# Turning self attention's output through DRAM and VectorE instead of TensorE, in a decoder layer on one core

## The chip, the core and the metric

The kernel runs on one core of one Trainium2 chip. The metric is the device time of one execution in microseconds; the median of 3 runs of the kernel before is 2142.93 (2141.88 to 2144.9). Its engines are TensorE (PE: matmuls; PEld: its weight loads), VectorE (DVE), ScalarE (ACT), GpSimd (POOL) and SyncE (SP), which only issues DMAs here. Each engine works through its own instructions in order, and waits on semaphores for the others.

## The reference

One decoder layer with its normalization behind each part, in fp32: self attention with relative positions, cross attention over a context, and a feed-forward part with its weights and hidden values rounded to 8 bits. x is (8, 512, 512). The first axis is the sequence here (8 positions) and the second is a batch of 512, so self attention has 8 keys for each of 16 heads of 32.

```python
qkv = x @ in_proj_weight.T + in_proj_bias
q, k, v = jnp.split(qkv, 3, axis=-1)             # each (t, b, h, d), t = 8, b = 512
p = (pos @ pos_proj_weight.T + pos_proj_bias).reshape(-1, h, d)
ac = jnp.einsum('tbhd,sbhd->bhts', q + r_w_bias, k)
bd = _rel_shift(jnp.einsum('tbhd,rhd->bhtr', q + r_r_bias, p))[..., :t]
attn = jax.nn.softmax((ac + bd) * scale, axis=-1)
ctx = jnp.einsum('bhts,sbhd->tbhd', attn, v).reshape(t, b, e)
x = _layernorm(x + ctx @ out_proj_weight.T + out_proj_bias)
...
x = _layernorm(x + cross_attention(ctx_2048, x, mask))
x = _layernorm(x + ffn(x))
```

The change concerns `ctx` and its product with `out_proj_weight`.

## The kernel before, in words

There are two stages, one after the other. The first does self attention and the keys and values of the context (1024 features) for cross attention; the second does cross attention and the feed-forward part. Only the first is touched.

**Self attention.** A loop over j = 0..3 takes 128 of the 512 batch rows at a time, one a partition, and within it loops over the 8 positions t. Keys (L232), queries (L373) and values (L410) come from TensorE through `project` (L214). As every batch row has its own 8 keys, scores and weighted sums are not matmuls but VectorE work: `pq` (L387) multiplies q by all keys and `sc` (L396) sums it, both in two halves (g) of eight heads. Behind the softmax (L415 to L427) comes the loop over t that the change is in. For each t, VectorE multiplies the values by the weights (`pv`, L436) and adds the eight products pairwise in three steps (L446, L449, L452), again in two halves; the last step writes one half of `ao`, 128 rows x 512 features. For the output product the features have to be on the partitions, so TensorE turns the four 128x128 blocks of `ao` (L457) into the PSUM bank `aot`, ScalarE copies them to `aoT` (L459), and TensorE multiplies by `w_o` into `po` (L462). x comes from DRAM as `r` (L471; a ring of 4) and GpSimd adds the bias (L472); VectorE adds `po` (L478) and takes statistics (L100, L101). After every fourth t the four rows are normalized (L111) and stored to `x1d` by ScalarE's queue; the ring's slots then load the next four x.

**Context.** Six of the eight contexts go in pairs (m = 0..2) through a Strassen-Winograd scheme with seven products a block instead of eight (L552; banks `py`, `pz`, `px` of the pool `a_kv`; sums of the operands on VectorE at L142 to L145, of the results at L594). In the first pass over the weights (keys) the sums of the context are also stored to DRAM (`td`, L529 and L530), in the second (values) they are loaded from there (L532, L533). Context chunks `ch` (L520) and `cl` stay in a ring of 8. Context 6 goes through the plain products `psk` (L160) and `psv` (L174), its weights `w6k` and `w6v` lying where k_all and v_all were: `w6v` can load once the last `pv` product has read v_all. Context 7 belongs to the second stage.

**What sets the order.** In the first stage the tile framework orders each engine's instructions by its own estimate of times: the context's matmuls are laid between those of self attention. All loads of the stage, and the stores to `td`, stand in one order on SP's queue, where a DMA that waits holds up those behind it. PSUM has 8 banks: 2 for projections, 1 each for `bd`, `aot` and `po`, 3 for the context.

In the second stage the order is written out by hand. It starts with the load of `x1Ts`, block-wise from `x1d` (`load_blocks`, L746), turned in place by VectorE (L752); its memory lies partly where a tile of context 6 was, which the last tile of `psv` reads. The products `psq` (L824) follow.

Of the kernel before, what the change touches and what calls it, by code (L numbers as in the profile page):

```python
# [9 lines left out]
F32 = mybir.dt.float32  # L10
# [5 lines left out]
PSUM = bass.MemoryType.PSUM  # L16

P = 128
E = 512
EC = E // P  # L20
# [22 lines left out]
def decoder_layer(  # L43
# [22 lines left out]
    nc = tc.nc  # L66
# [5 lines left out]
    ident = const.tile([P, P], F32, name="ident")  # L72
# [8 lines left out]
    def col(i):  # L81
# [3 lines left out]
    dram = ctx.enter_context(  # L85
        tc.tile_pool(name="dram", bufs=1, space=bass.MemoryType.DRAM)
    )
# [101 lines left out]
    with ExitStack() as ph:  # L189
# [5 lines left out]
        bo = wa.tile([P, E], F32, name="bo")  # L195
        ps_mm = ph.enter_context(tc.tile_pool(name="a_mm", bufs=2, space=PSUM))
        ps_bd = ph.enter_context(tc.tile_pool(name="a_bd", bufs=1, space=PSUM))
        ps_tr = ph.enter_context(tc.tile_pool(name="a_tr", bufs=1, space=PSUM))
        ps_o = ph.enter_context(tc.tile_pool(name="a_o", bufs=1, space=PSUM))
        ps_kv = ph.enter_context(tc.tile_pool(name="a_kv", bufs=3, space=PSUM))  # L200

        xtp = ph.enter_context(tc.tile_pool(name="xtp", bufs=8))
        kvp = ph.enter_context(tc.tile_pool(name="kvp", bufs=1))
        qp = ph.enter_context(tc.tile_pool(name="qp", bufs=2))
# [18 lines left out]
        def keys_of(j):  # L223

            k_all = kvp.tile([P, T, E], F32, tag="k", name=f"k{j}")
            xts = []
            for t in range(T):
                xt = xtp.tile([P, EC, P], F32, tag="xt", name=f"xt{j}_{t}")
                nc.sync.dma_start(xt, xT[t, j])
                xts.append(xt)  # L230
                ps = project(xt, 1, f"k{j}_{t}")
                nc.scalar.copy(k_all[:, t, :], ps)  # L232
            return xts, k_all
# [129 lines left out]
        for j in range(NJ):  # L363
            xts, k_all = first if j == 0 else keys_of(j)
            v_all = kvp.tile([P, T, E], F32, tag="v", name=f"v{j}")
            sc = kvp.tile([P, T, P], F32, tag="sc", name=f"sc{j}")

            for t in range(T):  # L370
                ps = project(xts[t], 0, f"q{j}_{t}")
                qw = qp.tile([P, E], F32, tag="qw", name=f"qw{j}_{t}")
                nc.vector.tensor_tensor(qw, ps, bqw, ALU.add)  # L373
                if t % 4 == 0:
                    bd = ps_bd.tile([P, 4, H1, T], F32, tag="bd", name=f"bd{j}_{t}")
                for e in range(EC):
                    nc.tensor.matmul(
                        bd[:, t % 4],
                        lhsT=xts[t][:, e, :],
                        rhs=gp[:, e, :, 7 - t : 15 - t],  # L380
                        start=(e == 0),
                        stop=(e == EC - 1),
                    )
                for g in range(2):
                    fs = slice(g * HW, (g + 1) * HW)
                    pr = prp.tile([P, HH, T, D1], F32, tag="pr", name=f"pq{j}_{t}_{g}")
                    nc.vector.tensor_tensor(  # L387
                        pr,
                        qw[:, fs]
                        .rearrange("p (h d) -> p h d", d=D1)  # L390
                        .unsqueeze(2)
                        .to_broadcast([P, HH, T, D1]),
                        k_all[:, :, fs].rearrange("p s (h d) -> p h s d", d=D1),
                        ALU.mult,
                    )
                    nc.vector.tensor_reduce(  # L396
                        sc[:, t, g * HH * T : (g + 1) * HH * T],
                        pr.rearrange("p h s d -> p (h s) d"),
                        AX.X,
                        ALU.add,  # L400
                    )
                if t % 4 == 3:
                    half = sc[:, t - 3 : t + 1, :].rearrange("p t s -> p (t s)")
                    nc.vector.tensor_tensor(
                        half, half, bd.rearrange("p t h s -> p (t h s)"), ALU.add
                    )

            for t in range(T):
                ps = project(xts[t], 2, f"v{j}_{t}")
                nc.scalar.copy(v_all[:, t, :], ps)  # L410


            for t in range(T):
                row = sc[:, t, :].rearrange("p (h s) -> p h s", s=T)
                nc.gpsimd.tensor_tensor(row, row, gc[:, :, 7 - t : 15 - t], ALU.add)  # L415
            sc3 = sc.rearrange("p t (h s) -> p (t h) s", s=T)
            red = sm.tile([P, T * H1], F32, tag="red", name=f"mx{j}")
            nc.vector.tensor_reduce(red, sc3, AX.X, ALU.max)
            nc.vector.tensor_tensor(
                sc3, sc3, red.unsqueeze(2).to_broadcast([P, T * H1, T]), ALU.subtract  # L420
            )
            nc.scalar.activation(sc3, sc3, AF.Exp, scale=1.0 / math.sqrt(D1))
            den = sm.tile([P, T * H1], F32, tag="red", name=f"den{j}")
            nc.vector.tensor_reduce(den, sc3, AX.X, ALU.add)
            rden = sm.tile([P, T * H1], F32, tag="rden", name=f"rden{j}")
            nc.vector.reciprocal(rden, den)
            nc.vector.tensor_tensor(  # L427
                sc3, sc3, rden.unsqueeze(2).to_broadcast([P, T * H1, T]), ALU.mult
            )

            for t in range(T):
                ao = qp.tile([P, E], F32, tag="ao", name=f"ao{j}_{t}")
                for g in range(2):
                    fs = slice(g * HW, (g + 1) * HW)
                    pr = prp.tile([P, T, HH, D1], F32, tag="pr", name=f"pv{j}_{t}_{g}")
                    nc.vector.tensor_tensor(  # L436
                        pr,
                        v_all[:, :, fs].rearrange("p s (h d) -> p s h d", d=D1),
                        sc[:, t, g * HH * T : (g + 1) * HH * T]
                        .rearrange("p (h s) -> p s h", s=T)  # L440
                        .unsqueeze(3)
                        .to_broadcast([P, T, HH, D1]),
                        ALU.mult,
                    )
                    pf = pr.rearrange("p s h d -> p s (h d)")
                    nc.vector.tensor_tensor(  # L446
                        pf[:, 0:4, :], pf[:, 0:4, :], pf[:, 4:8, :], ALU.add
                    )
                    nc.vector.tensor_tensor(  # L449
                        pf[:, 0:2, :], pf[:, 0:2, :], pf[:, 2:4, :], ALU.add  # L450
                    )
                    nc.vector.tensor_tensor(ao[:, fs], pf[:, 0, :], pf[:, 1, :], ALU.add)  # L452

                pt = ps_tr.tile([P, E], F32, tag="tr", name=f"aot{j}_{t}")
                for c in range(EC):
                    cs = slice(c * P, (c + 1) * P)
                    nc.tensor.transpose(pt[:, cs], ao[:, cs], ident)  # L457
                aoT = qp.tile([P, E], F32, tag="aoT", name=f"aoT{j}_{t}")
                nc.scalar.copy(aoT, pt)  # L459
                po = ps_o.tile([P, E], F32, tag="po", name=f"po{j}_{t}")  # L460
                for c in range(EC):
                    nc.tensor.matmul(  # L462
                        po,
                        lhsT=aoT[:, c * P : (c + 1) * P],
                        rhs=w_o[:, c, :],
                        start=(c == 0),
                        stop=(c == EC - 1),
                    )
                xin = rp.tile([P, E], F32, tag="r", name=f"r{j}_{t}")
                n0 = t * NB + j * P  # L470
                nc.sync.dma_start(xin, x[n0 : n0 + P, :])  # L471
                nc.gpsimd.tensor_tensor(xin, xin, bo, ALU.add)  # L472
                if t % 4 == 0:
                    mvs = sm.tile([P, 4, 2], F32, tag="mv1", name=f"mva{j}_{t}")
                    rts = []
                r = xin
                rts.append(r)
                nc.vector.tensor_tensor(r, po, r, ALU.add)  # L478
                stats_of(sm, mvs[:, t % 4, :], r, f"a{j}_{t}")
                if t % 4 == 3:  # L480
                    rs = rstd_of(sm, mvs, 4, f"a{j}_{t}")
                    for i in range(4):
                        normalize(rts[i], rts[i], mvs, rs, i)
                        nc.scalar.dma_start(x1d[t - 3 + i][j], rts[i])
# [141 lines left out]
        t = T - 2  # L626
# [735 lines left out]
```

## Time and profile before

| | |
|---|---|
| median of the runs | 2142.93 us |
| profiled execution, its own time | 2141.88 us |
| its span on the core | 2140.0 us |
| TensorE, busy | 2067.8 us (97%) |
| VectorE, busy | 1434.3 us (67%) |
| ScalarE, busy | 464.1 us (22%) |
| GpSimd, busy | 167.7 us (8%) |
| DMA, mean over the span | 119 GB/s |
| granted TensorE clock, mean | 0.989 |
| last `ao` of the first stage ends at | 833.70 us |
| load of `x1Ts` issued at | 887.70 us |

Busy time is the time in which at least one instruction of the engine runs; ends of matmuls are modelled, and consecutive ones overlap, so TensorE's share is an upper bound. A row of groups gives line, engine, operation, output and inputs by name, shape and count, then busy time and mean duration. An issue row of a DMA ends with its size and the median time from issue to landing. A row of waits reads: who waited for whom, total us, times, longest. A timeline row starts with start and duration.

### The profile page before, as it was taken

Reading aid. Unit: us, or ns where it says so; the run is one execution under the profiler, and the core shown is the slowest. Engines: PE = TensorE matmul, PEld = TensorE weight load, DVE = VectorE, ACT = ScalarE, POOL = GpSimd, SP = SyncE. Lnnn points to the kernel's source line nnn. Section 1 sums busy time; section 2 is a strip of 40 time slices with the busy share of each in tenths; the row PEclk is TensorE's granted clock in tenths of the full one; section 3 lists DMA queues with packets and bytes.
Section 4 is the critical chain, followed back from the end, with each engine's and each line's share of the span. In section 5 each row is a group of like instructions: output and inputs, shape, how many; then the busy total and the mean of one; then the engine's idle time right before and its main releaser. Section 6 shows DMA issues by size and latency. Waiting matters only on the chain.

```text
span 2140.0 us, 17293 instructions
## 1 busy us (share of the span) xinstructions
PE 2067.8 (97%) x5776; PEld 887.8 (41%) x5776; DVE 1434.3 (67%) x2290; ACT 464.1 (22%) x955; POOL 167.7 (8%) x148
## 2 busy tenths in 40 slices
PE   8999999999999999888999999999999999999998
PEld 5444444444444444333334443434444434443443
DVE  2999999999999996055763664845746648356332
ACT  3011101110110111122233232232332322323211
POOL 0100120011011001101101011010010100000000
PEclk9999999999999999999999999999999999999999
DMA  6510644134025345765484563844646537436200
GB/s 213 211 44 24 222 147 143 40 134 145 16 67 198 122 152 177 200 165 124 107 202 118 106 141 70 144 105 99 133 104 111 135 80 152 97 75 148 60 20 20
DMA packets 246201, 255.26 MB, mean 119 GB/s; under 512 B 141025, under 2 KB 161505, under 8 KB 246113
## 3 DMA queue, kind: packets, MB, share of 16 engines
q1 hardware_dynamic: 229888, 225.55, 41.3%
q10 hardware_dynamic: 16224, 28.61, 3.7%
q8 instruction: 46, 0.75, 0.1%
q14 instruction: 43, 0.34, 0.1%
HBM read 130.36 MB, written 56.62 MB: 87 GB/s over the span
## 4 chain that ended last, share of the span: by engine, by line
PE 65%; DVE 26%; DMA 5%; issue 2%; SPq 1%; POOL 1%; ACT 0%; ACTq 0%; DVEq 0%; POOLq 0%
PE h L1033 21%; PE pox L978 5%; PE s L844 5%; PE psq L824 5%; PE pox L966 5%; PE av L944 5%; DVE pv L436 5%; DVE sc L396 4%; PE o L1050 4%; DVE pq L387 4%; PE px L552 3%; DVE pv L446 3%; PE psk L160 3%; PE psv L174 2%; DVE pv L449 2%
## 5 line engine op out<-in xcount | busy, mean ns | idle before, releaser
L1033 PE MATMUL h<-x2T,w 128*128 128x512 f32 x1024 | 454.5, 599 | 4.4 <-DVE x2T L752 4.4
L1033 PEld LDWEIGHTS h<-x2T,w 128*128 128x128 f32 x1024 | 192.1, 191 | 263.2 <-issue 255.1
L859 DVE CUSTOM_DVE_ANT_0 pe<-s,mb 128x512 f32<-128x512 f32 x256 | 162.1, 681 | 206.7 <-PE s L844 206.7
L869 ACT ACTIVATE pe<-pe,nmax 128x512 f32<-128x512 f32 x256 | 182.2, 713 | 231.8 <-DVE nmax L859 230.0
L896 DVE STREAM_TRANSPOSE pb<-pe 128x512 f32<-128x512 f32 x256 | 159.5, 678 | 0.0
L1040 ACT ACTIVATE hq<-h,colv 128x512 fp8e4<-128x512 f32 x128 | 88.0, 687 | 296.8 <-PE h L1033 296.8
L436 DVE TENSOR_TENSOR pv<-v,sc 128x2048 f32<-128x2048 f32 x64 | 149.5, 2336 | 2.0
L387 DVE TENSOR_TENSOR pq<-qw,k 128x2048 f32<-128x2048 f32 x64 | 147.9, 2311 | 1.0
L396 DVE TENSOR_REDUCE sc<-pq 128x64 f32<-128x2048 f32 x64 | 146.0, 2282 | 1.4
L844 PE MATMUL s<-kT,qTx 64*128 64x512 f32 x512 | 130.0, 625 | 5.4 <-DVE nmax L859 5.3
L824 PE MATMUL psq<-x1Ts,w_tgt 128*128 128x512 f32 x256 | 119.2, 620 | 13.3 <-DVE x1Ts L752 13.3
L944 PE MATMUL av<-pT,vx 128*64 128x512 f32 x512 | 119.2, 608 | 7.0 <-DMA pT<-pb 5.7
L214 PE MATMUL ps_q<-w_in,xt 128*128 128x512 f32 x256 | 119.4, 598 | 0.4 <-DVE qw L373 0.4
L884 DVE TENSOR_SCALAR pe<-pe,rden 128x512 f32<-128x512 f32 x256 | 116.5, 497 | 4.5
L462 PE MATMUL po<-w_o,aoT 128*128 128x512 f32 x256 | 118.7, 607 | 0.0
L978 PE MATMUL pox<-w_xo,uT 128*128 128x512 f32 x256 | 115.2, 598 | 0.0
L966 PE MATMUL pox<-w_xo,x1Ts 128*128 128x512 f32 x256 | 115.0, 598 | 0.0
L214 PE MATMUL ps_k<-w_in,xt 128*128 128x512 f32 x256 | 115.0, 599 | 0.0
L1050 PE MATMUL o<-w2q,hq 128*128 128x512 fp8e4 x512 | 114.1, 379 | 0.0
L214 PE MATMUL ps_v<-w_in,xt 128*128 128x512 f32 x256 | 112.0, 594 | 0.0
L985 DVE TENSOR_TENSOR x<-pox,x 128x512 f32<-128x512 f32 x32 | 22.1, 692 | 106.4 <-PE pox L978 68.5
L552 PE MATMUL px<-tx,w 128*128 128x512 f32 x192 | 89.0, 595 | 3.0 <-DVE st L594 3.0
(147 smaller groups left out, 2136.8 us busy)
## 6 DMA issues: line engine op xcount, KB each, us to landing
pT<-pb SPq DMA_DIRECT2D x512, 128.0 KB, 2.3
ch<-in_ctxT_dram SPq DMA_DIRECT2D x24, 512.0 KB, 5.7
td<-tx SPq DMA_DIRECT2D x12, 768.0 KB, 6.0
tx<-td SPq DMA_DIRECT2D x12, 768.0 KB, 9.3
xt<-in_xT_dram SPq DMA_DIRECT2D x32, 256.0 KB, 2.7
r<-in_x_dram SPq DMA_DIRECT2D x32, 256.0 KB, 3.7
x1d<-r ACTq DMA_DIRECT2D x32, 256.0 KB, 2.5
x1Ts<-x1d SPq DMA_DIRECT2D x32, 256.0 KB, 5.9
```

Of the source, the lines that this page charges most:

```text
L214: nc.tensor.matmul(ps, lhsT=xt[:, e, :], rhs=w_in[:, e, part * E : (part + 1) * E], start=(e == 0), stop=(e == EC - 1),)
L387: nc.vector.tensor_tensor(pr, qw[:, fs] .rearrange("p (h d) -> p h d", d=D1) .unsqueeze(2) .to_broadcast([P, HH, T, D1]), k_all[:, :, fs]. ...
L396: nc.vector.tensor_reduce(sc[:, t, g * HH * T : (g + 1) * HH * T], pr.rearrange("p h s d -> p (h s) d"), AX.X, ALU.add,)
L436: nc.vector.tensor_tensor(pr, v_all[:, :, fs].rearrange("p s (h d) -> p s h d", d=D1), sc[:, t, g * HH * T : (g + 1) * HH * T] .rearrange( ...
L824: nc.tensor.matmul(ps, lhsT=w_tgt[:, e, o * P : (o + 1) * P], rhs=x1T[t][:, e, :], start=(e == 0), stop=(e == EC - 1),)
L844: nc.tensor.matmul(ps[:, h, :], lhsT=qT[t][half[h], c, j * P : (j + 1) * P], rhs=kT[t, c][half[h], :], start=True, stop=True,)
L869: nc.scalar.activation(pe, pe, AF.Exp, bias=nmax[:, h : h + 1], scale=-1.0, accum_out=den[:, h : h + 1],)
L944: nc.tensor.matmul(av[half[h], :], lhsT=v[t, c][:, s, half[h]], rhs=pT[t, c][:, :, :, s, h].rearrange("p g i q -> p (g i) q"), start=(s == 0),
L966: nc.tensor.matmul(po, lhsT=x1T[t][:, e, j * P : (j + 1) * P], rhs=w_xo[:, e, :], start=(e == 0), stop=False,)
L978: nc.tensor.matmul(po, lhsT=uT[t][:, e, j * P : (j + 1) * P], rhs=w_xo[:, EC + e, :], start=False, stop=(e == EC - 1),)
L1033: nc.tensor.matmul(ps, lhsT=w1[0][:, e, n * P : (n + 1) * P], rhs=x2T[t][:, e, :], start=(e == 0), stop=(e == EC - 1),)
L1050: nc.tensor.matmul(po, lhsT=hq[t][:, c, j * P : (j + 1) * P], rhs=w2q[:, c, :], start=(c == 0), stop=(c == HC - 1),)
```

## The change

In the loop over t of the weighted sums, `ao` is stored to a DRAM tile of its own (`aod`), and loaded back in four DMAs, all on SP's queue. The DMA for a fills the partitions 32a to 32a + 31 with the features of that quarter of each 128-feature chunk, taken in 32x32 blocks: 512 runs of 32 elements, 128 B each. One VectorE instruction then transposes each 32x32 block of `aoT` in place, which completes the turn, and the output product reads `aoT` as before. `aoT` gets three buffers instead of two. TensorE's transposes, their PSUM bank and ScalarE's copy go; the bank goes to the pool of the context's products, which has four instead of three. In the changed program the lines behind the edit lie seven further (output product L469, transpose L466, store L457, block loads L460).

```diff
-        ps_tr = ph.enter_context(tc.tile_pool(name="a_tr", bufs=1, space=PSUM))
         ps_o = ph.enter_context(tc.tile_pool(name="a_o", bufs=1, space=PSUM))
-        ps_kv = ph.enter_context(tc.tile_pool(name="a_kv", bufs=3, space=PSUM))
+        ps_kv = ph.enter_context(tc.tile_pool(name="a_kv", bufs=4, space=PSUM))
...
-                pt = ps_tr.tile([P, E], F32, tag="tr", name=f"aot{j}_{t}")
-                for c in range(EC):
-                    cs = slice(c * P, (c + 1) * P)
-                    nc.tensor.transpose(pt[:, cs], ao[:, cs], ident)
-                aoT = qp.tile([P, E], F32, tag="aoT", name=f"aoT{j}_{t}")
-                nc.scalar.copy(aoT, pt)
+                aod = dram.tile([P, E], F32, name=f"aod{j}_{t}")
+                nc.sync.dma_start(aod, ao)
+                aoT = qp.tile([P, E], F32, tag="aoT", bufs=3, name=f"aoT{j}_{t}")
+                for a in range(4):
+                    nc.sync.dma_start(
+                        aoT[32 * a : 32 * a + 32].rearrange(
+                            "p (c g e) -> p c g e", c=EC, e=32
+                        ),
+                        aod.rearrange("(g r) (c a e) -> a r c g e", r=32, a=4, e=32)[a],
+                    )
+                nc.vector.transpose(aoT, aoT)
                 po = ps_o.tile([P, E], F32, tag="po", name=f"po{j}_{t}")
```

## Prediction

> **What bounds the kernel now.** I read the page's first two parts, then the waits and windows of the first 900 us (the change sits there), then the timeline of a few tiles, and last the order in which the changed program's instructions stand on each engine, beside that of the old one.
>
> The page says TensorE is 97% busy, which hides where the change falls. In the 40 slices (53.5 us each) VectorE is full from the second to the fifteenth and thins out after:
>
> ```profile
> PE   8999999999999999888999999999999999999998
> DVE  2999999999999996055763664845746648356332
> ```
>
> Windows, whose columns are length, then busy time and instructions of PE, PEld, DVE, ACT and POOL, PEclk, DMA share and GB/s:
>
> ```profile
> 53.00:838.00 785.00, 757.26 (x2011) 344.17 (x2011) 740.54 (x664) 95.61 (x153) 73.69 (x65) 1.00 0.34 119
> 838.00:896.00 58.00, 55.64 (x130) 24.32 (x128) 3.66 (x8) 7.51 (x11) 3.44 (x2) 1.00 0.69 207
> ```
>
> VectorE works 740.5 of 785 us. TensorE's 757 overstates it: a 128x512 matmul record lasts 0.6 us but the next starts 0.43 us later, so the stage's 1600 records of that size (768 of L214, 256 of L462, 576 of L552) are 688 us, the 256 of L377 at 0.11 another 28. VectorE is the tighter engine; of its 44 us of idle time 31 have a name and lie before the last ao, half of them inside the softmax (columns: total, times, longest):
>
> ```profile
> DVE den L424 <- ACT sc L422: 8.6, 4, 2.5
> DVE mx L418 <- POOL sc L415: 7.1, 4, 1.8
> DVE r L478 <- PE po L462: 5.9, 2, 5.1
> DVE r L478 <- POOL r L472: 5.2, 4, 1.7
> DVE st L594 <- PE px L552: 4.8, 4, 3.6
> ```
>
> From 838 to 896 only TensorE works, on context 6 (psk, psv). The last ao ends at T = 833.70; the load of x1Ts that opens the second stage is issued at 887.70, T + 54.0. Since the orders from psq on are the same in both programs, the change is worth what it does to T plus what it does to that tail.
>
> **The change part by part.**
>
> *Taken off TensorE:* 128 transposes of 128x128, a record every 0.11 us: 14 us. With them go its weight loads' waits for ao (27.8 us) and for aoT (15.4 us). TensorE is not what T waits for, so I book nothing, except that VectorE's waits on px and po may shrink: -2 us of the 5.6 that they make without the 5.1 that fell after T. *Taken off ScalarE:* 32 copies of 587 ns, on an engine at 22%: nothing. *The fourth bank* lets products start earlier: nothing while VectorE sets T.
>
> *Added to VectorE:* 32 transposes of 128x512, 31 of them before T in the new order. The nearest row is the same operation on the same shape:
>
> ```profile
> L752 DVE STREAM_TRANSPOSE x1Ts<-x1Ts x32: 667/670/711, 898.3 to 1797.7; 128x512 f32<-128x512 f32 x32
> ```
>
> A rule speaks for the full price: the Trainium skill, "VectorE: DVE Perf Modes", section on the DRAIN, says the next operation does not start until the pipe has emptied. That makes 31 x 0.67 = 20.8 us. The trace disagrees where an independent operation is put between two dependent ones, which is where most of these stand:
>
> ```profile
> 372.72 1.23 DVE L446 TENSOR_TENSOR pv<-pv 128x1024 f32<-128x1024 f32 x1
> ...
> 375.17 2.29 DVE L436 TENSOR_TENSOR pv<-v,sc 128x2048 f32<-128x2048 f32 x1
> 377.38 0.68 DVE L478 TENSOR_TENSOR r<-po,r 128x512 f32<-128x512 f32 x1
> 377.98 1.22 DVE L446 TENSOR_TENSOR pv<-pv 128x1024 f32<-128x1024 f32 x1
> ```
>
> L446 starts 2.81 us after its L436 with r between and 2.33 without (370.39 to 372.72): r starts 0.08 before its predecessor ends and the next 0.08 before r does, so its 0.68 costs 0.48. About 23 transposes stand so (0.48); 8 stand beside another inserted operation, where only the later overlap helps (0.60). I take 31 x 0.51 = +15.8 us.
>
> *Moved past T:* r, its statistics and aggregate for j=3, t=6 come after the last ao now (before, at 829.6). By the same timeline the three together cost 10.49 - 9.54 = 0.95 us a t: -1.0 us.
>
> *Added to SP's queue:* 32 stores of 256 KB and 128 block loads of 64 KB, each first load waiting for its store to land, with everything behind it on SP waiting too. Rows for 256 KB each (last column: us from issue to landing), the first two in runs of 2 KB, the third in runs of 128 B like the block loads:
>
> ```profile
> xt<-in_xT_dram SPq DMA_DIRECT2D x32, 256.0 KB, 2.7
> ...
> x1d<-r ACTq DMA_DIRECT2D x32, 256.0 KB, 2.5
> x1Ts<-x1d SPq DMA_DIRECT2D x32, 256.0 KB, 5.9
> ```
>
> The Trainium skill, "DMA: Bandwidth & Descriptors", Specifications, wants at least 512 B a run for full rate; the loads have 128 B. It gives no price, the rows do: 256 KB in 128 B runs land 3.2 us later than in 2 KB runs, a quarter of it is 0.8; raw<-vd, 64 KB in 512 B runs, lands in 2.2 us and takes 0.44 to issue. So a block load is 3.0 us and a turned tile is ready 2.5 + 4 x 0.44 + 3.0 = 7.3 us after ao. From above: four issues at x1Ts's own median, 1.4 us, and its 5.9 give 14.0 us. I take 7.3, as 64 KB is nearer to raw's size.
>
> What hides it: in the new order 11.6 us of VectorE's operations or more stand between an ao and its transpose (13.9 to 16.3 for about half), about 11 by the overlap above. At 7.3 us it costs nothing; past 11 the transpose holds up every pv product behind it in VectorE's order. From the transpose to the add of r there are 4.65 us, and po takes 3.7 from a free TensorE: covered.
>
> Where other issues stand between, I work out what is late:
> - j=0, t=4: SP's order has two context loads (ch, cl) between the store and the block loads; cl waits for the buffer's last reader, seven products (6.0 us) behind po of t=3 (3.5). So it issues 9.7 us after the transpose of t=3 and lands 6.6 later by its row, the block loads behind it no sooner: 16.3, and VectorE asks at 13.8: +2.5 us.
> - j=1, t=4: six stores of sums to td (3.75 MB; 1.2 us each to issue) stand before the load of r of t=4, which also needs a normalized row's store. Counted from the sum that frees the first store, the normalized row is stored at 13, r lands 3.7 later and has bo added in 1.7: 18.4; VectorE asks at 15.8: +2.6.
> - the other loads of r behind SP's new waits, and po where TensorE is just inside a matmul: +2, my estimate.
>
> Together with the -2 above: +5 us. From below -9 (no new stall, and the 5.6 of px and po and the 3.3 of tx gone), from above 93, as 31 times 14 - 11.
>
> *The tail.* The new order puts the output product of t=6 (j=3) right behind its transpose, 0.45 us before T, and then, up to the matmul that frees x1Ts's memory (the first of psv's last tile), 4 + 1 + 18 + 4 + 10 + 25 = 62 matmuls at 0.86, 53.4 us, which is 53.0 after T instead of 54.0: -1.0. Inside it, the last tile's block loads stand behind 2 MB of w6v and 2 MB of w_src: at their rows' 8.8 and 14.4 us to land, w_src issued at T + 4.4 when its memory is free, it is ready by about T + 20, and TensorE reaches it at T + 19.4 after 18 psk matmuls. Those are its cover; past them each late us counts. I put 0, at most 8.
>
> Sum: 15.8 - 1.0 + 5 - 1.0 = +18.8 us. The profiled execution took 2141.88 us, 1.9 of it outside the span of 2140.0; its span becomes 2158.8 and its time 2160.7. The median of the runs shown is 1.05 higher: 2142.93 + 18.8 = **2161.7 us**, say 2162, 0.9% slower.
>
> **Rivals.**
> - *The chain from ao to the turned tile is late.* Against: 7.3 us fits into 11. For: SP takes one thing at a time, and x1Ts landed in 13.3 us at worst. At 12.5 us a tile, 31 x 1.5 = 46 more: 2208; at 14 it is 2255.
> - *The transposes fall into idle time.* VectorE idles 44.5 us in the stage. If all ran in it and no new stall came, it is 2142.9 + 0 - 1 - 1 = 2141, and 2132 with the old waits of px, po and tx gone as well (-9), faster. It decides once gaps take more than 13.8 of the 15.8 us, or more than 4.8 with those waits gone. Against: 15.7 us of the idle time are the softmax's own, where only t=7's transposes could stand, and the order has them behind later pq products instead.
> - *No change to speak of.* Half the price hidden (8 us) and no new stall (0): 2142.9 + 8 - 1 - 1 = 2149 is still slower; it takes 6 us of the old waits gone as well to come to 2143.
>
> **How the numbers follow.** My case 0.70 (own range 2152 to 2180: the stalls from -3 to +20, the tail to +4), the late chain 0.18, idle time 0.05, no change 0.07. Within 0.2% (4.3 us) is what a measurement of this kernel can't tell from no change: faster 0.05, same 0.07, slower 0.88. The range of 8 in 10 starts at 2148 (stalls at -9) and leaves out the upper part of the late chain: 2148 to 2205.
>
> **What would show it.** Right: VectorE's busy time rises by 16 to 21 us before the last ao, which ends near 854; pv keeps 2.3 us; idle time of VectorE before aoT below 10 us in sum; block loads landing in about 3 us; x1Ts issued 53 us after the last ao; everything behind it as before. Wrong: waits of VectorE on DMA aoT in tens of us (the chain is late), TensorE idle before the last po (the tail), or a transpose at its full 0.67 in the spacing of pv (+5).

## The result, and the profile after

The changed kernel takes 2170.64 us (median of 4 runs, 2169.73 to 2172.72) against 2142.98 beside it: ratio 1.0132, 95% interval 1.0120 to 1.0144, so 27.7 us slower. 2162 was forecast, with 2148 to 2205 as the range. The profiled execution has a span of 2168.2 us against 2140.0.

Where the prediction looked, the new profile mostly agrees with it. VectorE's and TensorE's rows of the 40 slices:

```profile
PE   8999799998998989997899999999999999999998
DVE  2999899998999998055664574754835748456232
```

The slices hardly tell the kernels apart. The waits of VectorE up to the last ao (total, times, longest; the rows of the stage itself):

```profile
DVE den L423 <- ACT sc L421: 8.6, 4, 2.5
DVE r L485 <- POOL r L479: 8.4, 3, 5.0
...
DVE r L485 <- PE po L469: 5.6, 3, 3.8
```

No transpose of VectorE waits for the block loads before the last ao: the trip is covered for VectorE. Its pieces come out close to the rows of before. The transpose and the DMA issue rows (last column: KB each, then us from issue to landing):

```profile
L466 DVE STREAM_TRANSPOSE aoT<-aoT x32: 673/703/711, 176.6 to 878.0; 128x512 f32<-128x512 f32 x32
```

```profile
aod<-ao SPq DMA_DIRECT2D x32, 256.0 KB, 2.0
aoT<-aod SPq DMA_DIRECT2D x128, 64.0 KB, 2.8
```

With a median of 0.63 us for an issue, the trip is 2.0 + 4 x 0.63 + 2.8 = 7.3 us, the number that the prediction used. From the end of ao to the landing of its last block load it is 7.3 us at the median of the 32 tiles too, over 9 in eight of them and 16.3 at worst. T, the end of the last ao, went from 833.70 to 861.58 (forecast: near 854), and the load of x1Ts is issued at 914.97, T + 53.4 (forecast: 53.0). One could stop here: T moved, the tail stayed, the end follows. The experiments show that this reading is wrong.

What differs when one looks at TensorE instead? Its windows from 53 us to the first psq (length, busy time of PE, PEld, DVE, ACT, POOL, granted clock, DMA share, GB/s), before:

```profile
53.00:899.00 846.00, 812.91 (x2140) 368.49 (x2139) 744.91 (x674) 103.16 (x164) 77.12 (x67) 0.99 0.37 126
```

and after:

```profile
53.00:926.10 873.10, 811.69 (x2014) 363.08 (x2012) 767.81 (x705) 84.59 (x132) 76.46 (x67) 0.98 0.45 141
```

TensorE lost its 128 transposes and is busy as long as before; its idle time rose from 33.1 to 61.4 us. psq starts 27.1 us later, 28.3 of it idle time. The largest of its waits, of before:

```profile
PE aot L457 <- DVE ao L452: 12.3, 12, 2.1
```

and of after, where TensorE waits 30.7 us for turned tiles, 7.1 in one piece:

```profile
PE po L469 <- DVE aoT L466: 30.7, 13, 7.1
PE px L559 <- DVE st L601: 8.4, 6, 3.5
PE py L559 <- DMA w<-in_w_srcT_dram: 5.6, 1, 5.6
PE pz L559 <- DVE tx L142: 5.2, 2, 2.7
```

Waits for the tile thus make 18.4 of the 28.3 us; waits for sums that VectorE makes of the context (`tx`) and of the results (`st`) make most of the rest.

### The profile page after: what moved, and what is told of

The parts are those of the page before. It is cut to its first block, busy times and chain, and to the rows that moved or that the text cites. A ratio compares the mean times of both kernels' runs of the same rounds, so it can differ in the third digit from the quotient of the medians.

```text
span 2168.2 us, 17315 instructions
## 1 busy us (share of the span) xinstructions
PE 2068.0 (95%) x5648; PEld 883.3 (41%) x5648; DVE 1454.7 (67%) x2322; ACT 445.2 (21%) x923; POOL 167.0 (8%) x148
## 4 chain that ended last, share of the span: by engine, by line
PE 62%; DVE 28%; DMA 4%; issue 3%; SPq 1%; ACT 1%; POOL 0%; DVEq 0%; ACTq 0%; POOLq 0%
PE h L1040 21%; DVE sc L395 6%; DVE pq L386 6%; PE pox L985 5%; PE s L851 5%; PE psq L831 5%; PE pox L973 5%; PE av L951 5%; PE o L1057 4%; DVE pv L435 4%; PE psk L160 2%; DVE pv L445 2%; PE px L559 2%; PE psv L174 2%; PE po L469 2%
## 5 line engine op out<-in xcount | busy, mean ns | idle before, releaser
L469 PE MATMUL po<-w_o,aoT 128*128 128x512 f32 x256 | 127.4, 644 | 30.9 <-DVE aoT L466 30.7
L479 POOL TENSOR_TENSOR r<-r,bo 128x512 f32<-128x512 f32 x32 | 51.3, 1626 | 569.5 <-DMA r<-in_x_dram 418.2
```

## The experiments

All runs in one table. "T" is the end of the last ao, "psq" the start of the second stage's first product; busy and idle time are TensorE's from 53 us to psq; all of the profiled execution.

| kernel | median us | T | psq | busy | idle |
|---|---|---|---|---|---|
| before | 2142.98 | 833.7 | 899.1 | 812.9 | 33.1 |
| after | 2170.64 | 861.6 | 926.1 | 811.7 | 61.4 |
| before, plus a transpose on VectorE | 2140.33 | 848.3 | 899.0 | 814.2 | 31.8 |
| before, TensorE's transposes twice | 2152.19 | 825.2 | 908.6 | 826.0 | 29.6 |
| before, without TensorE's transposes | 2130.24 | 834.1 | 887.6 | 800.1 | 34.5 |
| the same, with the fourth bank | 2145.62 | 843.5 | 901.7 | 806.9 | 41.7 |
| after, three banks | 2200.25 | 843.9 | 957.5 | 813.2 | 91.3 |
| after, without the transpose | 2192.16 | 834.7 | 948.6 | 815.8 | 79.8 |
| after, without the trip | 2139.13 | 857.0 | 896.4 | 803.5 | 39.8 |
| after, trip's DMAs issued, not awaited | 2150.39 | 856.0 | 907.8 | 806.2 | 48.6 |
| after, turn written a tile later | 2166.23 | 856.7 | 921.8 | 810.9 | 57.9 |
| after, trip on ScalarE's queue | 2169.15 | 880.5 | 923.9 | 810.3 | 60.6 |
| both of these | 2161.99 | 874.6 | 918.4 | 809.3 | 56.0 |
| three banks, only t = 0..3 through DRAM | 2148.27 | 833.7 | 900.7 | 804.7 | 43.0 |

Median less psq is 1241 to 1248 us in every row: the second stage is the same, and psq decides. T does not: the kernel with T at 825.2 is slower than before, the one with 848.3 is not, and from T to psq it is anything from 39 us to 114. The six kernels in which the product of every tile waits for the trip take 2162 to 2200 us, all in which none does 2130 to 2152.

### VectorE's transposes alone

```diff
+                spare = qp.tile([P, E], F32, tag="spare", bufs=1, name=f"spare{j}_{t}")
+                nc.vector.transpose(spare, ao)
                 pt = ps_tr.tile([P, E], F32, tag="tr", name=f"aot{j}_{t}")
```

> The kernel before, with one more VectorE transpose of ao for each t into a spare tile that nothing reads; TensorE's path stays. Theory (VectorE sets the stage's end, a transpose costs it 0.48 to 0.60 us): 31 x 0.51 = 16, so 2159 us. Rival 1 (each instruction costs its full 0.68): 2143 + 21 = 2164. Rival 2 (the price of the change lies in the trip through DRAM, and VectorE has room): 2143 to 2146.

2140.33 us, ratio 0.9985 (0.9978 to 0.9992): the prediction's theory is out. VectorE's busy time in the stage rose by 17.7 us and T by 14.6, as that theory says, and psq did not move (899.06 to 899.03). Around and behind T TensorE has psk and psv to do, 124 matmuls at 0.43 or 53 us of them after T in the kernel before, and only psv needs anything of VectorE's loop: w6v's memory. That load was issued at 845.9 and landed 8.7 us later; TensorE came to psv at 866.2. T had slack.

### The trip without the turn, and the turn without the trip

Two edits of the changed kernel, the first without the transpose:

```diff
-                nc.vector.transpose(aoT, aoT)
```

> The changed kernel with the trip through DRAM, but without VectorE's transpose: the output product reads the blocks unturned. Theory: 16 us less than the changed kernel, 2155 us, the rest of the loss being delays of the trip and of the new order. Rival (the trip is the price): 2167 to 2171.

2192.16 us, 1.0222 (1.0205 to 1.0239), although VectorE has 20 us less to do in the stage than in the changed kernel and T is at 834.7 (the 32x32 blocks stay unturned in it). The output product starts 10.6 us after ao on average, earlier than in the changed kernel, and yet TensorE idles longer: it waits 22.2 us for loads of the context (`ch`, `tx`; 7.5 in before). How late the product is does not rank the kernels by itself. The second has the transpose and no trip, so the blocks are turned but not exchanged:

```diff
-                aod = dram.tile([P, E], F32, name=f"aod{j}_{t}")
-                nc.sync.dma_start(aod, ao)
...
-                nc.vector.transpose(aoT, aoT)
+                nc.vector.transpose(aoT, ao)
```

> The changed kernel without the store to DRAM and the block loads: VectorE transposes ao's 32x32 blocks straight into aoT. The output leaves out the exchange of blocks. Theory: VectorE's 16 us stay, the delays that the trip brought (about 10 us: r's loads, the late half of w7) go: 2143 + 16 = 2159 us. Rival (the trip is the price): 2143 to 2147.

2139.13 us, 0.9983 (0.9976 to 0.9990). Here the turned tile is ready one transpose after ao, and the output product starts 1.2 us after ao on average (1.7 before, with TensorE's transposes and ScalarE's copy). In the changed kernel it is 14.3 us. So the trip costs, 31.5 us between these two kernels, and the transposes don't. TensorE waits for turned tiles here too, though:

```profile
PE po L460 <- DVE aoT L457: 19.0, 12, 4.9
```

against 30.7 us in the changed kernel. Of the 21.6 us of idle time between these two, 11.7 are such waits.

### Three banks

```diff
-        ps_kv = ph.enter_context(tc.tile_pool(name="a_kv", bufs=4, space=PSUM))
+        ps_kv = ph.enter_context(tc.tile_pool(name="a_kv", bufs=3, space=PSUM))
```

> The changed kernel with three banks for the context's products instead of four (the eighth bank unused). Theory: the bank is worth nothing, as VectorE sets the stage's end: 2168 to 2174 us. Rival (the new order of the start, 3.9 us, and of w7's loads, 4.7 us, comes from the fourth bank): 2162.

2200.25 us, 1.0266 (1.0250 to 1.0281), 29.6 above the changed kernel, where at most 3.4 were expected; with T 17.7 us earlier. It shows best where the time goes. Four windows of 55 us, each around the end of one loop of sums (from 40 us before its last ao to 15 behind):

```profile
215.00:270.00 55.00, 36.76 (x75) 15.11 (x74) 49.56 (x56) 2.36 (x4) 5.15 (x4) 0.81 0.70 227
416.00:471.00 55.00, 34.38 (x68) 13.85 (x67) 53.34 (x62) 3.64 (x5) 7.21 (x4) 0.78 0.65 209
612.00:667.00 55.00, 37.44 (x71) 14.76 (x70) 53.09 (x57) 3.82 (x6) 6.60 (x4) 0.84 0.65 193
804.00:859.00 55.00, 41.16 (x87) 16.90 (x86) 43.37 (x53) 3.24 (x5) 6.67 (x4) 0.88 0.79 238
```

TensorE is busy 149.7 of these 220 us. The sum of the same windows of before:

```profile
sum 220.00, PE 209.71 PEld 92.95 DVE 199.78 ACT 24.45 POOL 23.01; mean PE 52.43 PEld 23.24 DVE 49.95 ACT 6.11 POOL 5.75
```

and of after:

```profile
sum 220.00, PE 187.10 PEld 78.13 DVE 194.34 ACT 17.07 POOL 23.60; mean PE 46.77 PEld 19.53 DVE 48.59 ACT 4.27 POOL 5.90
```

So of the 28.3 us of idle time that after has more than before, 22.6 lie there, and in the three-bank kernel 60.0, against 58.2 over the whole stretch to psq. TensorE's two largest waits of the three-bank kernel, up to psq, are

```profile
PE po L469 <- DVE aoT L466: 51.2, 15, 15.4
PE px L559 <- DMA cl<-in_ctxT_dram: 16.6, 2, 12.6
```

so not all of it is waiting for turned tiles. The 12.6 us end at 259.67, at the end of the first loop: that cl was issued on SP's queue at 255.59, right behind a store of ao that had waited there for ao until 255.22. The context's products that don't get done there are done behind T: the groups of TensorE from 844 to 957 in the three-bank kernel have, beside psk and psv,

```profile
L559 PE MATMUL px<-tx,w 128*128 128x512 f32 x32 | 15.0, 606 | 0.0
L559 PE MATMUL px<-cl,w 128*128 128x512 f32 x28 | 12.8, 593 | 0.0
```

where the kernel before has, from 834 on, psk, psv, one output product with two transposes, and seven matmuls of px left. That is the stretching "tail".

### TensorE's work up and down

Each transpose of the kernel before done twice:

```diff
                     nc.tensor.transpose(pt[:, cs], ao[:, cs], ident)
+                    nc.tensor.transpose(pt[:, cs], ao[:, cs], ident)
```

> The kernel before, with TensorE's 128 transposes of ao done twice into the same bank. Nothing else changes; VectorE's work is the same. Theory now (TensorE is what ends the first stage; psq starts when TensorE has done its work and its waits): the work without transposes was 803.6 us of TensorE's busy time up to psq, with them 812.9, so a second set costs 9 us by that, 14 by 128 times 0.107: 2152 to 2157. Prediction's view (VectorE sets the end through T, TensorE's transposes are worth nothing): 2143 to 2145.

and not at all:

```diff
-                    nc.tensor.transpose(pt[:, cs], ao[:, cs], ident)
-                aoT = qp.tile([P, E], F32, tag="aoT", name=f"aoT{j}_{t}")
-                nc.scalar.copy(aoT, pt)
...
-                        lhsT=aoT[:, c * P : (c + 1) * P],
+                        lhsT=ao[:, c * P : (c + 1) * P],
```

> The kernel before without TensorE's transposes and ScalarE's copy: the output product reads ao unturned (so the output product is of the wrong operand; that turn is left out). The bank is left unused, VectorE has the same work. Theory now (TensorE ends the stage): 9 to 14 us of transposes go, the waits of TensorE on ao stay: 2129 to 2134. Prediction's view (VectorE's T and 53 us behind it): T at most 2 us earlier, 2141 to 2143.

2152.19 us (1.0047, 1.0030 to 1.0064) and 2130.24 (0.9941, 0.9926 to 0.9956). 9.6 us more, 12.4 us less, both within what TensorE as the bound gives, and psq moves by the same (+9.5, -11.5). The twice-done transposes even let T come 8.5 us earlier. What the first stage lasts is TensorE's work together with TensorE's idle time. (In the second kernel the output product also starts 5 us before ao is complete, on its first half; idle time hardly changes, 34.5 against 33.1.)

Then the second of them with the free bank given to the context:

```diff
-        ps_kv = ph.enter_context(tc.tile_pool(name="a_kv", bufs=3, space=PSUM))
+        ps_kv = ph.enter_context(tc.tile_pool(name="a_kv", bufs=4, space=PSUM))
```

> As the run without TensorE's transposes and ScalarE's copy (the output product reads ao unturned, the turn is left out), with the free bank given to the context's pool, four instead of three. Theory (the fourth bank lets TensorE run ahead where it would wait; with short waits there is little to gain): 2125 to 2131. Prediction's view (a fourth bank is worth nothing): 2129 to 2131. If the bank is worth by itself what it was under the trip (30 us): near 2113, the floor that VectorE's T sets.

2145.62 us (1.0011, 1.0000 to 1.0023): the bank costs 15.4 us here, where it was expected to be worth 0 to 5, and under the trip it saved 29.6. Idle time is 7.2 us more, busy time 6.8. A bank has no price of its own: with each edit the framework writes another order of TensorE's instructions, and these two orders differ by more than anything that one would book for a bank. Why it ranks them so, the runs don't show.

### Is it SP's queue, or the late product?

The changed kernel with its store and block loads still issued, into a tile that nothing reads, while VectorE turns ao directly:

```diff
-                aoT = qp.tile([P, E], F32, tag="aoT", bufs=3, name=f"aoT{j}_{t}")
+                aoT = qp.tile([P, E], F32, tag="aoT", name=f"aoT{j}_{t}")
+                spare = qp.tile([P, E], F32, tag="spare", bufs=1, name=f"spare{j}_{t}")
                 for a in range(4):
                     nc.sync.dma_start(
-                        aoT[32 * a : 32 * a + 32].rearrange(
+                        spare[32 * a : 32 * a + 32].rearrange(
...
-                nc.vector.transpose(aoT, aoT)
+                nc.vector.transpose(aoT, ao)
```

> The kernel without the trip in its path (VectorE turns ao straight into aoT, so the exchange of blocks is left out), but with the store and the four block loads still issued on SP's queue, into a spare tile that nothing reads. It parts the trip's 31.5 us (2170.6 against 2139.1 without the trip) into the DMAs' presence on SP's queue and the time for which the output product waits. Theory (the chain: the product comes late and stands in TensorE's order ahead of other work): 2139 to 2146. Rival (SP's queue: waiting DMAs of the trip hold up the loads of w7, x and the context): 2158 to 2171. Both: between, and the share above 2139 is the queue's.

2150.39 us (1.0030, 1.0018 to 1.0042): between the two. Of the trip's 31.5 us, 11.3 come with the DMAs alone and 20.2 when the product has to wait for them. (The order is not the same in the two, and aoT has one buffer less, so the split is no finer than the 15 us that an order has been seen to do.)

Two remedies. The turn, the product and what follows written behind the next tile's sums:

```diff
-                nc.vector.transpose(aoT, aoT)
...
+                if late:
+                    finish(*late)
+                late = (t, aoT)
+            finish(*late)
```

> The changed kernel with one thing moved: the turn, the output product and what follows of tile t are written behind the sums of tile t+1, so that the trip through DRAM has a tile's sums of VectorE (about 11 us) as cover in the order of both engines. Store, loads, queue and banks as in the changed kernel. Theory now (the 61 us of TensorE's idle time come from output products that stand in TensorE's order ahead of the arrival of their aoT): idle falls to about 30 us, the clock drops behind the gaps go with it, psq at 888 to 899 (not under T + 38.5), 2131 to 2143. Prediction's view (32 transposes on VectorE and its T set the end): still 2158 to 2167. Rival, the trip's DMAs hold up SP's queue and with it the other loads: still 2160 to 2171, as all of them are still there.

The trip on another queue:

```diff
-                nc.sync.dma_start(aod, ao)
+                nc.scalar.dma_start(aod, ao)
...
-                    nc.sync.dma_start(
+                    nc.scalar.dma_start(
```

> The changed kernel with the store of ao and the four block loads on ScalarE's DMA queue instead of SP's. Rival (SP's queue: the trip's DMAs wait there and hold up loads of w7, x and the context): most of the 28 us come back, 2145 to 2152. Theory now (the chain from ao to the turned tile is as long as before, and TensorE meets it): only the waits for w7 and the context of some 8 us come back, and ScalarE's results wait behind the queued DMAs: 2160 to 2172. Prediction's view: 2160 to 2170.

And both:

> Both remedies at once: the turn and the output product one tile later, and the trip's DMAs on ScalarE's queue. One alone left 2166.2 and 2169.2. If the later turn failed only because SP's queue held up x and the context behind the trip, and ScalarE's queue failed only because the turn met the late loads, then both together give 2140 to 2152. If the trip costs TensorE its cover in another way (its order around the end of each loop of sums), 2158 to 2168.

2166.23, 2169.15 and 2161.99 us (1.0105, 1.0126, 1.0091, each interval within 0.002 of it). The deferred kernel is 23 us above what the theory gave it, both remedies together are 10 above the case that they work; only ScalarE's queue did what the theory had for it, and the deferred kernel lies where both of its rivals had it. Writing the turn later changed little because the framework had put it there already: from the end of ao to the start of the turn it is 12.6 us at the median in the changed kernel and 12.8 in the deferred one. ScalarE's queue took the waits from SP and gave VectorE new ones, since the block loads land late there; VectorE's waits in that kernel begin with

```profile
DVE aoT L466 <- DMA aoT<-aod: 18.9, 5, 5.5
```

which SP's queue did not have. So neither remedy brings the time back. The timeline of the changed kernel at the end of the first loop (start, duration) shows what happens there. First the DMAs of t = 6 and 7 and the load behind them on SP's queue, then VectorE, then TensorE:

```profile
247.95 0.32 SPq L457 DMA_DIRECT2D aod<-ao  x1
...
250.16 2.61 SPq L460 DMA_DIRECT2D aoT<-aod  x4
261.61 0.34 SPq L457 DMA_DIRECT2D aod<-ao  x1
...
267.19 0.63 SPq L529 DMA_DIRECT2D cl<-in_ctxT_dram  x1
```

```profile
261.16 0.43 DVE L451 TENSOR_TENSOR ao<-pv 128x256 f32<-128x256 f32 x1
261.62 2.29 DVE L386 TENSOR_TENSOR pq<-qw,k 128x2048 f32<-128x2048 f32 x1
263.83 0.70 DVE L466 STREAM_TRANSPOSE aoT<-aoT 128x512 f32<-128x512 f32 x1
...
277.39 0.68 DVE L142 TENSOR_TENSOR tx<-cl 128x512 f32<-128x512 f32 x1
```

```profile
259.46 2.74 PE L559 MATMUL pz<-tx,w 128*128 128x512 f32 x6
264.59 3.70 PE L469 MATMUL po<-w_o,aoT 128*128 128x512 f32 x8 [2.39 <-DVE aoT L466]
275.36 1.22 PE L469 MATMUL po<-w_o,aoT 128*128 128x512 f32 x1 [7.07 <-DVE aoT L466]
```

t = 6 is stored at 247.95, its last block load is issued by 252.77 and lands within 4.0 us (the longest in this stretch), and it is turned only at 263.83, behind the sums of t = 7, four operand sums and the first pq product of the next j. TensorE has run out of other work in its order at 262.2, and after that product stands 7 us before the one of t = 7. From 248 to 278 VectorE is busy 28.9 of 30 us and TensorE 16.2. The cover that lets VectorE run on keeps the product from TensorE.

That is one part. TensorE's order has no other work there because the next context products lack their operands, and SP's queue has a share in that. After 252.8 it stood 8.8 us at the store of t = 7, waiting for ao; cl, behind the store and its block loads, landed at 271.4, and the first operand sum made after that (`tx`) ends at 278.07. The next context product in TensorE's order, at 281.14, takes a `tx` too, so by this order TensorE would most likely have stood until 278 without the output product as well. The same end shows the queue's share between kernels. TensorE's idle time in the 55 us around it is 3.5 us in before, 4.3 without the trip, 11.6 with DMAs that nobody awaits, 18.6 in the changed kernel and 8.2 with the trip on ScalarE's queue, where other waits took the place of those saved. The late product and the held-up loads both cost; how much each does is open, as every one of these kernels has its own order.

### Only where TensorE has other work

If the ends of the loops are where the trip costs, the trip may stay in the first half of each loop:

```diff
+                if t >= 4:
+                    pt = ps_tr.tile([P, E], F32, tag="tr", name=f"aot{j}_{t}")
+                    for c in range(EC):
+                        cs = slice(c * P, (c + 1) * P)
+                        nc.tensor.transpose(pt[:, cs], ao[:, cs], ident)
+                    nc.scalar.copy(aoT, pt)
+                else:
```

> The changed kernel with three banks for the context, in which only the tiles t = 0..3 of each loop are turned through DRAM and VectorE, and t = 4..7 through TensorE and ScalarE as before (the fourth bank is theirs again). The run with three banks and all tiles through DRAM took 2200.25 with 91.3 us of TensorE's idle time, of which about 67 us lie within the last 35 us of each loop of sums and just behind it. Theory (the trip costs where TensorE has no other work left in its order, at the ends of the loops): idle falls to 35 to 45 us, half the transposes are saved (5 us), psq at 896 to 910: 2137 to 2152. Rival (each trip costs alike, wherever it is): half of the 57 us above before stay, 2165 to 2178.

2148.27 us (1.0028, 1.0011 to 1.0046), 52.0 below the three-bank kernel with all tiles through DRAM, where the rival had half of 57 us left. The windows around its loop ends sum to

```profile
sum 220.00, PE 207.23 PEld 89.49 DVE 205.39 ACT 29.60 POOL 28.97; mean PE 51.81 PEld 22.37 DVE 51.35 ACT 7.40 POOL 7.24
```

207.2 us of TensorE against 149.7. With half of the trips, all in the first half of the loops, 6 us of the price are left. That agrees with the ends of the loops as the place of the cost, within what a new order can do. It doesn't tell the late product from the queue, as both are gone from the ends. It is the fastest of the kernels with the trip that compute the whole layer, and still slower than before; no run that computes the whole layer beats the kernel before by more than the 0.15% of the first experiment, which only adds to it.

## Why the prediction was right or wrong

**The sum came near for a wrong reason, by luck.** 18.8 us were forecast, 27.7 measured, inside the range. The path "VectorE's T, plus a tail of 53 us" is not what sets psq.

**The step that failed is the choice of the tighter engine**: "a 128x512 matmul record lasts 0.6 us but the next starts 0.43 us later, so the stage's 1600 records of that size (768 of L214, 256 of L462, 576 of L552) are 688 us, the 256 of L377 at 0.11 another 28. VectorE is the tighter engine." The pitch is right, the count is not. In the same window (53 to 838) the groups list 694 records of L214, 255 of L462, 668 of L552 and 12 others, 1629 at 0.43 = 700.5 us; 254 of L377 are 27.9, and the 128 transposes, left out, 14.1. That is 742.5 us of TensorE against 740.5 of VectorE: level, and TensorE alone has another 53 us of psk and psv to do after it, half of which (psk) needs nothing from VectorE's loop. With the row of windows read as it stands (757 of 785 us) TensorE would have been the bound.

**"TensorE is not what T waits for, so I book nothing"**: true of T, and wrong for the end. The kernel without the transposes is 12.4 us faster, near the 14 us that the prediction counted for them. The relief was received, and given back: psq's +27.1 us are -14.1 of transposes, +15.3 of slower matmuls (the last section has the count) and +28.3 of idle time, to within 2.4 us.

**31 x 0.51 = +15.8 us on VectorE**: somewhat low as a size, and worth nothing in the time. The first experiment's transposes add 17.7 us to VectorE's busy time up to T, 0.57 each, between the 0.51 and the full 0.67 (20.8 us). In the changed kernel it is +18.1, where 14.8 were forecast with what moves past T. The Trainium skill, "VectorE: DVE Perf Modes", section on the DRAIN, from which the prediction took the full price, goes on that a next operation that is not held (made to wait for those before it) starts earlier; the prediction's own rows agree (0.48 us for r's 0.68). The rival that the transposes fall into idle time named the right outcome for them (2141 forecast, 2140.33 and 2139.13 measured) and the wrong place: they fell into the slack behind T.

**"What hides it: ... 11.6 us of VectorE's operations or more stand between an ao and its transpose. ... At 7.3 us it costs nothing"**: the 7.3 us are right, and VectorE did not wait. But with what stands between, the product comes 14.3 us behind ao for TensorE, where it came at 1.7. The late-chain rival asked only at which length VectorE would wait (12.5, 14 us); the price came at 7.3, on the other engine.

**The new stalls, +5**: VectorE's idle time up to T rose by 9.8 us, about twice what was booked and in part elsewhere. Of the stalls worked out, r at j = 1, t = 4 came (1.9 us at 445, 2.6 forecast), and the late tile at j = 0, t = 4 did not; there r waited 5.0 us for x at 233. The second weights' operand sums waited 5.7 at 510 (two of their four loads stood behind loads of x on SP), po 3.8 at 794.

**"The fourth bank lets products start earlier: nothing"**: wrong in size and not of one sign: -29.6 us under the trip, +15.4 without transposes or trip.

**The tail**: 53.4 us, 53.0 forecast, and w6v in front of the last block loads cost nothing (landed at 866.9, used at 893.3). But it is no constant: from T to the issue of x1Ts it is 28 to 101 us in these kernels.

## What to carry to other kernels

Before a change moves work from one engine to another, add up both engines' work to the point that decides, from the groups' counts and the real pitch, with everything that only one of them has to do at the end; when they come out level, neither may be booked at nothing. A transfer that is "hidden" behind one engine's work is hidden for that engine only: ask when the consumer on the other engine gets its operand, and whether it has anything else in its order at that place, above all at the ends of loops; and ask which loads stand behind a DMA that waits for a late result. Where a framework orders the instructions, every edit buys a new order, which was worth up to 30 us here; a part's price is known only from the kernel with that part alone.

## What was not expected of the hardware

TensorE can pay for a gap twice. In the three-bank kernel, after 15.4 us without work, eight matmuls of one output product take 6.08 us, against 3.60 where there is no gap:

```profile
450.00 6.08 PE L469 MATMUL po<-w_o,aoT 128*128 128x512 f32 x8 [15.39 <-DVE aoT L466]
```

The granted clock of that stretch was 0.62:

```profile
435.00:460.00 25.00, 6.08 (x9) 2.38 (x9) 23.47 (x22) 0.00 (x0) 7.21 (x4) 0.62 0.54 159
```

The Trainium skill, "TensorE: Matmul & The Clock Gate", Part 1, has the rule: about 3.4 us without work halve the clock until about 3.4 us of work have passed. By that the loss would be an estimated 1.7 us a gap; here it was 2.5. In length the trace does not agree. In the changed kernel a product takes 5.40 us after a gap of 2.13 us, with TensorE busy for 10 us before it:

```profile
164.74 10.46 PE L213 MATMUL ps_k<-w_in,xt 128*128 128x512 f32 x24
177.34 5.40 PE L469 MATMUL po<-w_o,aoT 128*128 128x512 f32 x8 [2.13 <-DVE aoT L466]
```

Eight matmuls after one of 3.53 us, at 452.35, took the usual 3.70, at a granted clock of 1.00. So a gap's length alone does not tell here whether it slows what follows.

Over the stage, to psq, the 128x512 matmul records of more than 0.65 us exceed the usual 0.59 by 23.6 us in the changed kernel, 15.6 without the trip and 8.3 in before: 15.3 us more than before, in matmuls that the change did not touch, about as much as its saved transposes had brought.
